# Inverse DFT over W of a two-layer convolution block: even frequencies by the parity of k2 over a quarter of the row, sums on GpSimd

## Chip, cores and metric

The kernel runs on one core of one Trainium2 chip. The metric is the device time of one execution in microseconds (us). All arithmetic is in float32. TensorE is called PE in the profile (its weight loads are listed apart as PEld), VectorE is DVE, ScalarE is ACT, GpSimd is POOL, SyncE is SP.

## The reference

The input `x` is a batch of 4 images of 512 x 512 pixels with 16 channels. Two layers are applied, each to a group-normalised copy of its input and with a residual sum.

```python
# layer 0
X = rfft2(gn(x), s=(1024, 1024));  Y = einsum('...hwi,ijhw->...hwj', X, H_full)
x = x + irfft2(Y, s=(1024, 1024))[..., :512, :512, :]
# layer 1
x = x + conv3x3_cosine_arccos(gn(x))      # 3x3, 16 to 16 channels, divided by norms
```

`H_full` is a filter made from two small polynomials. Only the last transform of layer 0 matters here: the inverse DFT over W. It turns 512 complex frequencies per image row (of a transform of length 1024) into 512 real pixels.

## The kernel before

The work goes through five phases in order of time: the filter (`filter_phase`, with the statistics of the first normalisation beside it), the forward transform over W, the mixing of channels per frequency (`conv_phase`, by far the longest), and then `last_phase`. This starts with the stage that the change touches, the inverse DFT over W, and goes on with layer 1.

**The stage.** It is the `with ExitStack() as inner` block of `last_phase`, and it makes 256 tiles of 128 rows by 512 pixels. The outer loop over `n` (16 steps) loads eight inputs `yt0` to `yt7` of 1 MB each through SP's DMA queue, from two buffers per input (`i_y`, `bufs=2`), so the loads for step n+2 wait until PE has done with step n. The inner loop over `m` (16 steps) makes one tile. The frequencies lie in eight chunks of 128, which are cosine chunks kc = 0 to 3 and sine chunks kc = 4 to 7; in each four the first two are even frequencies `2*k2` (with k2 sorted into even and odd ones) and the last two are odd frequencies.

The tile is made from the symmetry about the middle of the row. Eight matmuls (L1141) of 128 x 128 weights, which are the data, by 128 x 256 moving columns, which are the constant `inv`, put the sum over cosines in `po[:, 0]` and the sum over sines in `po[:, 1]`, each for the left half of the row. ACT copies the sine half to SBUF (L1146, `od`). DVE adds the two plus a bias for the left half (L1148), and subtracts them for the right half, written backwards (L1149). ACT's queue then issues the store of the tile to the DRAM array `yw_d` (L1153). `po` has four PSUM buffers, `od` and `yo` four SBUF buffers.

**The work beside it.** The generator `prepare` reads the result back for the second normalisation. One place of it is a 128 x 128-pixel patch: it loads the patch of the original image (`p_x`, 1 MB) and of `yw_d` (`p_y`, two halves of 0.5 MB), adds them on POOL (L1071, two additions per place), takes statistics on DVE (L1067, 16 instructions per place), and stores the sum to `t_d` (1 MB). There are 64 places, 16 per image. A place of image 0 needs rows that steps n = 0 to 7 of the stage write. In the program's text, `next(beside)` is called from step n = 9 on, and later once per unit of layer 1; a scheduler then lays all instructions out in one fixed order per engine, and moves places forward where it believes an engine to be free. An engine executes its own queue strictly in that order.

**Layer 1.** It has 256 units of 128 rows x 32 columns. Each uses PE (L1183, L1209, L1279, L1287), ACT (L1191 to L1315), DVE (L1297, L1331 to L1334) and POOL (L1320, L1325, L1339) in turn; the remaining places of `prepare` run in between. L1339 runs once per unit and so counts the units in the trace.

Of the kernel before, what the change touches and what calls it, by code (L numbers as in the profile page):

```python
# [40 lines left out]
F32 = mybir.dt.float32  # L41
AF = mybir.ActivationFunctionType
ALU = mybir.AluOpType
AX = mybir.AxisListType
PSUM = bass.MemoryType.PSUM

P = 128
N = 512
# [22 lines left out]
def constants():  # L71

    c = {}
# [21 lines left out]
    for cc in range(2):  # L95
        taps = (back * (1, 1j)[cc]).reshape(N, S, 8)
        for plane in range(2):
            v = np.einsum("kse,sr->kre", (taps.real, taps.imag)[plane], over_s)
# [8 lines left out]
    for r in range(33):  # L107
# [5 lines left out]
        for part in range(2):  # L113
# [6 lines left out]
            else:  # L120
                v = -(sig.real @ np.sin(f_all))
# [16 lines left out]
    a = fwd.reshape(2, 4, P, 2, P).transpose(4, 3, 1, 0, 2).copy()  # L138
# [5 lines left out]
    own = np.pad(own, ((0, 0), (0, 9 * 64 - own.shape[1]))).reshape(2, 9, 64)  # L144
    c["own"] = np.tile(own.transpose(1, 0, 2).reshape(-1), (P, 1))
    inv = fwd * np.where(f > 0, 2.0, 1.0)[:, None] / (2 * N)
    c["inv"] = inv.reshape(8, P, 256).transpose(1, 0, 2).reshape(P, -1)
    c["ident"] = np.eye(P)

    def turn(n, of):  # L150
# [15 lines left out]
    for s0 in range(4):  # L166
        for cx in range(2):
            for c2 in range(2):
                n = gg[:, None] * s0 + 4 * gg[:, None] * s1[None, :] + 32 * (cx + c2)
# [20 lines left out]
def load_const(nc, pool, cst, name, shape=None):  # L190
    src = cst[name]
    t = pool.tile(list(src.shape), F32, name=f"c_{name}")
    nc.sync.dma_start(out=t, in_=src)
    return t


def dram(t, row, offset, *dims):

    pitch = t.shape[1]
    lead = [[pitch, t.shape[0]]] if row is None else []  # L200
    return bass.AP(tensor=t.tensor, offset=t.offset + (row or 0) * pitch + offset,
                   ap=lead + [list(d) for d in dims])
# [759 lines left out]
def last_phase(tc, cst, x, y_d, yw_d, t_d, kern, bias, radius, out):  # L962
    nc = tc.nc
    with ExitStack() as ctx:
# [22 lines left out]
        bias_y = cp.tile([P, 1], F32, name="l_bias_y")  # L987
# [132 lines left out]
        with ExitStack() as inner:  # L1120
            ip = inner.enter_context(tc.tile_pool(name="i_const", bufs=1))
            yp = inner.enter_context(tc.tile_pool(name="i_y", bufs=2))
            op = inner.enter_context(tc.tile_pool(name="i_o", bufs=4))
            ps = inner.enter_context(tc.tile_pool(name="i_ps", bufs=4, space=PSUM))
            inv = load_const(nc, ip, cst, "inv").rearrange("p (k n) -> p k n", k=8)
            for n in range(16):
                b2, half, s8 = n // 8, n // 4 % 2, n % 4
                yt = []
                for kc in range(8):
                    t = yp.tile([P, 4, 2, 2, P], F32, name=f"yt{kc}")  # L1130
                    at = (64 * half + 32 * (kc // 4) + 16 * b2 + 4 * s8) * 4 * P
                    nc.sync.dma_start(
                        out=t.rearrange("p a o h x -> p (a o h x)"),
                        in_=dram(y_d[kc % 4], None, at, [1, 16 * P]),
                    )
                    yt.append(t)
                for m in range(16):
                    s1, odd, bh = 4 * s8 + m // 4, m // 2 % 2, m % 2
                    po = ps.tile([P, 2, 256], F32, name="po")
                    for kc in range(8):  # L1140
                        nc.tensor.matmul(  # L1141
                            po[:, kc // 4], yt[kc][:, m // 4, odd, bh, :], inv[:, kc, :],
                            start=(kc % 4 == 0), stop=(kc % 4 == 3),
                        )
                    od = op.tile([P, 256], F32, name="od")
                    nc.scalar.copy(od, po[:, 1])  # L1146
                    o = op.tile([P, N], F32, name="yo")
                    nc.vector.scalar_tensor_tensor(o[:, :256], po[:, 0], bias_y, od, ALU.add, ALU.add)  # L1148
                    nc.vector.scalar_tensor_tensor(o[:, 256:][:, ::-1], po[:, 0], bias_y, od,  # L1149
                                                   ALU.add, ALU.subtract)  # L1150

                    h0 = 8 * (4 * s1 + 2 * half + odd)
                    nc.scalar.dma_start(out=yw_d[2 * bh + b2][:, h0 : h0 + 8, :], in_=o)  # L1153
                    if n >= 9 and m % 2 == 1:
                        next(beside, None)
# [232 lines left out]
def body(tc, ins, cst, out):  # L1388
    g_d = [tc.dram_tile([P, G_ROW + PITCH], F32, name=f"g_d{r}") for r in range(4)]
    x_d = [tc.dram_tile([P, X_ROW + PITCH], F32, name=f"x_d{r}") for r in range(4)]  # L1390
    y_d = [tc.dram_tile([P, Y_ROW + PITCH], F32, name=f"y_d{r}") for r in range(4)]
    yw_d = [tc.dram_tile([C, N, N], F32, name=f"yw_d{b}") for b in range(B)]
    t_d = [[tc.dram_tile([N, P, C], F32, name=f"t_d{b}_{w}") for w in range(4)] for b in range(B)]
    with tc.tile_pool(name="s_mv", bufs=2 * B) as mp:
        mvs = []
        with tc.tile_pool(name="s_in", bufs=1) as xp:
            beside = image_stats(tc, xp, mp, ins["x"], mvs)
            filter_phase(tc, cst, ins["L0_conv_h0"], ins["L0_conv_numerators"][0],
                         ins["L0_conv_denumerator"], g_d, beside)
            for _ in beside:  # L1400
                pass
        forward_phase(tc, cst, ins["x"], mvs, x_d)
    conv_phase(tc, cst, g_d, x_d, y_d)
    last_phase(tc, cst, ins["x"], y_d, yw_d, t_d, ins["L1_conv_kernel"], ins["L1_conv_bias"],
               ins["L1_conv_radius"], out)
# [6 lines left out]
def build(inputs, body=body):  # L1412
    import concourse.bacc as bacc

    nc = bacc.Bacc("TRN2", target_bir_lowering=False, num_devices=1)
    arrays, ins, cst = {}, {}, {}
    for name in _INS:
        a = np.ascontiguousarray(inputs[name])
        arrays[f"in_{name}"] = a
        ins[name] = nc.dram_tensor(f"in_{name}", a.shape, F32, kind="ExternalInput").ap()  # L1420
    for name, a in constants().items():
        arrays[f"k_{name}"] = a
        cst[name] = nc.dram_tensor(f"k_{name}", a.shape, F32, kind="ExternalInput").ap()
    out = nc.dram_tensor("out", (B, N, N, C), F32, kind="ExternalOutput").ap()
    with tile.TileContext(nc) as tc:  # L1425
        body(tc, ins, cst, out)
    return nc, arrays
# [8 lines left out]
```

## Times and profile before

| what | value |
|---|---|
| median of 3 runs | 16473.95 us (16464.4 to 16498.5) |
| profiled execution, its own time | 16489.29 us |
| span of the profiled execution | 16487.4 us, granted PE clock 0.972 |
| PE busy in the span | 15039.9 us (91%) |
| first and last L1141 matmul | 13694.0 us and 14696.4 us |
| L1141 | 4096 instructions (two per float32 matmul), 923.0 us busy |
| L1148 and L1149 on DVE | 256 each, 480 and 475 ns |
| L1146 on ACT | 256, 372 ns |
| L1071 on POOL, 128 x 1024 | 128, 2848 ns |
| L1067 on DVE, 128 x 128 | 1024, 366 ns |
| first and last L1339 | 14780.8 us and 16481.6 us |

The page gives busy times over the whole span, where the stage is only 6% of it. The stage is therefore read from answers of the trace for stretches of time: busy time of each engine in each stretch, the granted PE clock, the busy share of the DMA engines, the waits by what ended them, and the timelines of single engines. A busy time of a matmul includes the tail of the pipeline, so the pace of a run of matmuls is read from the starts of neighbouring groups and not from the mean duration of one.

### The profile page before, as it was taken

Reading aid. Unit: us, or ns where it says so; the run is one execution under the profiler, and the core shown is the slowest. Engines: PE = TensorE matmul, PEld = TensorE weight load, DVE = VectorE, ACT = ScalarE, POOL = GpSimd, SP = SyncE. Lnnn points to the kernel's source line nnn. Section 1 sums busy time; section 2 is a strip of 40 time slices with the busy share of each in tenths; the row PEclk is TensorE's granted clock in tenths of the full one; section 3 lists DMA queues with packets and bytes.
Section 4 is the critical chain, followed back from the end, with each engine's and each line's share of the span. In section 5 each row is a group of like instructions: output and inputs, shape, how many; then the busy total and the mean of one; then the engine's idle time right before and its main releaser. Section 6 shows DMA issues by size and latency. Waiting matters only on the chain. (4 is left out here: it accounts for less than half of the span.)

```text
span 16487.4 us, 538106 instructions
## 1 busy us (share of the span) xinstructions
PE 15039.9 (91%) x232588; PEld 11221.5 (68%) x232588; DVE 10549.6 (64%) x20763; ACT 8870.6 (54%) x17007; POOL 10203.4 (62%) x9645
## 2 busy tenths in 40 slices
PE   7999999999988889898988899888889998988898
PEld 5555555554567777677777777777777777777787
DVE  8999999974545555555555555555555552447877
ACT  4666666653345555555555555555555551027888
POOL 7777777763356666666666666666666660237766
PEclk8999999999999999999999999999999999989999
DMA  4888888888888888888888888888888886885531
GB/s 139 241 244 247 240 243 248 240 244 250 251 282 328 324 326 330 317 327 329 328 329 317 326 328 327 317 318 324 324 326 329 326 321 232 313 279 167 167 110 67
DMA packets 2914640, 4542.92 MB, mean 276 GB/s; under 512 B 126114, under 2 KB 2094460, under 8 KB 2801422
## 3 DMA queue, kind: packets, MB, share of 16 engines
q1 hardware_dynamic: 2703070, 3836.37, 67.9%
q0 software_dynamic: 172336, 605.00, 9.5%
q10 hardware_dynamic: 36864, 67.13, 1.2%
q8 instruction: 1833, 30.03, 0.7%
q14 instruction: 537, 4.40, 0.1%
HBM read 3030.71 MB, written 1477.31 MB: 273 GB/s over the span
## 5 line engine op out<-in xcount | busy, mean ns | idle before, releaser
L828 PE MATMUL pg<-c_dg,g 64*128 64x128 f32 x32832 | 2838.7, 290 | 344.4 <-ACT gh L728 192.2
L844 PE MATMUL pm<-xe,gh 128*32 128x64 f32 x131328 | 2380.2, 222 | 520.0 <-issue 299.3
L844 PEld LDWEIGHTS pm<-xe,gh 128*32 128x32 f32 x131328 | 2001.1, 110 | 1113.6 <-issue 891.7
L828 PEld LDWEIGHTS pg<-c_dg,g 64*128 64x128 f32 x32832 | 2277.5, 189 | 690.3 <-issue 248.1
L873 DVE TENSOR_TENSOR z<-zq,pz 128x256 f32<-128x256 f32 x2052 | 859.5, 419 | 2634.6 <-ACT zq L872 2567.4
L726 DVE COPY gh<-pg 128x512 f32<-128x512 f32 x2046 | 1408.2, 688 | 1208.9 <-PE pg L828 1205.8
L458 PE MATMUL pt<-ev_in,c_todd 128*128 128x512 f32 x4096 | 1927.5, 609 | 16.2 <-DMA ev_in<-g_d 16.2
L797 POOL TENSOR_TENSOR xu<-xe,c_late 128x256 f32<-128x256 f32 x2052 | 1391.7, 702 | 808.5 <-ACT xe L728 791.2
L388 DVE RECIPROCAL dn<-dn 128x256 f32<-128x256 f32 x1024 | 1722.8, 1724 | 17.6
L728 ACT COPY yf<-pm 128x512 f32<-128x512 f32 x2046 | 1211.4, 592 | 886.9 <-PE pm L844 873.2
L389 POOL TENSOR_TENSOR sp<-m,dn 128x512 f32<-128x512 f32 x1024 | 1300.9, 1271 | 592.4 <-DVE dn L388 552.0
L808 ACT COPY xe<-xl 64x1024 f32<-64x1024 f32 x513 | 538.7, 1050 | 1877.9 <-POOL xl L799 1877.8
L728 ACT COPY gh<-pg 128x512 f32<-128x512 f32 x2058 | 1200.2, 583 | 368.8 <-PE pg L828 365.7
L865 PE MATMUL pz<-c_ident,yf 128*128 128x128 f32 x8208 | 1371.7, 290 | 24.2 <-issue 10.8
L458 PEld LDWEIGHTS pt<-ev_in,c_todd 128*128 128x128 f32 x4096 | 728.2, 190 | 920.6 <-issue 792.3
L417 ACT COPY st<-pg 128x256 f32<-128x256 f32 x2048 | 616.8, 391 | 1301.5 <-PE pg L406 1301.3
L406 PEld LDWEIGHTS pg<-c_dinv,sp 64*128 64x128 f32 x16384 | 1005.5, 196 | 442.2 <-ACT sp L394 232.6
L799 POOL TENSOR_TENSOR xl<-xl,xu 128x1024 f32<-128x1024 f32 x513 | 1209.5, 2358 | 40.2
L406 PE MATMUL pg<-c_dinv,sp 64*128 64x128 f32 x16384 | 1108.2, 287 | 60.2 <-ACT sp L394 44.6
L881 POOL TENSOR_TENSOR zd<-z 128x512 f32<-128x512 f32 x513 | 653.7, 1274 | 765.4 <-DVE z L873 765.3
L1279 PE MATMUL pc<-l_band,xn 128*128 128x160 f32 (+2 forms) x6144 | 1076.2, 333 | 51.7 <-DVE e_o L1334 51.7
L913 POOL DMA_DIRECT2D y_d<-yo x511 | 296.5, 580 | 1325.0 <-ACT yo L728 1299.8
(211 smaller groups left out, 30193.2 us busy)
## 6 DMA issues: line engine op xcount, KB each, us to landing
xe<-xf_d SPq DMA_DIRECT2D x1026, 1536.0 KB
g<-g_d SPq DMA_DIRECT2D x511, 1024.0 KB
g_d<-st SPq DMA_DIRECT2D x256, 1024.0 KB
ev_in<-g_d SPq DMA_DIRECT2D x1024, 256.0 KB
g_d<-ot SPq DMA_DIRECT2D x1024, 256.0 KB
xf_d<-xe POOLq DMA_DIRECT2D x513, 448.0 KB, 8.2
xf_d<-xl POOLq DMA_DIRECT2D x513, 448.0 KB, 5.4
x_d<-xo SPq DMA_DIRECT2D x128, 1024.0 KB
```

Source lines behind the costliest of these rows:

```text
L388: nc.vector.reciprocal(dn, dn)
L389: nc.gpsimd.tensor_mul(w["sp"][:, v], w["m"][:, v], bc(dn, 2, [P, 2, 2, P]))
L406: nc.tensor.matmul(pg[u][:, n, k].rearrange("p a x -> p (a x)"), w["sp"][q, n, k, c, :], dinv[q, 2 * kp + k, c, :], start=(c == 0), stop=( ...
L458: nc.tensor.matmul(pt, todd[:, c, kc, hh * P : hh * P + P], ev[:, kc, c], start=(kc == 0), stop=(kc == 1),)
L726: nc.vector.tensor_copy(dst, src)
L728: nc.scalar.copy(dst, src)
L797: nc.gpsimd.tensor_mul(u[:, :, h, c], xe[:, :, h, 1 - c], bc(late[:, 1 + c], 2, [P, F, 2]))
L799: nc.gpsimd.tensor_add(xl.rearrange("p f h c k -> p (f h c k)"), xl.rearrange("p f h c k -> p (f h c k)"), u.rearrange("p f h c k -> p (f ...
L828: nc.tensor.matmul(pg[c][:, j % 4], g[half, j], dg[half], start=True, stop=True)
L844: nc.tensor.matmul(pm[32 * q : 32 * q + 32, g % 8], gh[:, f].rearrange("p c j -> p (c j)"), xe[:, :, f].rearrange("p t h c k -> p t (h c k ...
L865: nc.tensor.transpose(pz[:, t % 4].rearrange("p v q x -> p (v q x)"), y[:, at].rearrange("p g x -> p (g x)"), ident)
L1279: nc.tensor.matmul(pc[:, lo:hi, :].rearrange("p w j -> p (w j)"), xns[q][:, h * P + dh : h * P + dh + P], bands[dh][:, o : o + hi - lo, :] ...
```

## The change

The constant `inv` is split into an odd part, for both halves of the 256 columns, and an even part, for the first 128 columns only. The left half of the row is cut once more about its own middle: of the even frequencies, those with even k2 repeat mirrored and those with odd k2 repeat mirrored with the opposite sign (for cosines, and the other way round for sines). So 128 columns are computed for each parity.

Per tile there are now four matmuls of 128 columns, each by itself (`pe`, four results of 128 columns: parity by cosine or sine), and four of 256 columns for the odd frequencies (`po`, two results accumulated over two chunks). ACT copies all of `pe` to SBUF (`ye`, 512 columns). POOL adds and subtracts the two parities (`yq`, two instructions of 256 columns). DVE adds the odd sums in `po` to `yq` in place (512 columns), and then makes the tile with two instructions of 256 columns as before, which read `yq` from SBUF. The odd part of the constant and the second quarter of the even results are stored mirrored, so the output pattern has two stretches of 128 columns per instruction. `pe` and `po` have three PSUM buffers each, `ye` and `yq` three SBUF buffers each, `yo` keeps four.

```diff
     inv = fwd * np.where(f > 0, 2.0, 1.0)[:, None] / (2 * N)
-    c["inv"] = inv.reshape(8, P, 256).transpose(1, 0, 2).reshape(P, -1)
+    inv = inv.reshape(2, 4, P, 2, P).transpose(2, 0, 1, 3, 4).copy()
+    inv[:, :, 2:, 1] = inv[:, :, 2:, 1, ::-1]
+    inv[:, 1, 2:, 1] *= -1
+    c["inv"] = np.concatenate([inv[:, :, 2:].reshape(P, -1), inv[:, :, :2, 0].reshape(P, -1)], 1)
...
-            op = inner.enter_context(tc.tile_pool(name="i_o", bufs=4))
-            ps = inner.enter_context(tc.tile_pool(name="i_ps", bufs=4, space=PSUM))
-            inv = load_const(nc, ip, cst, "inv").rearrange("p (k n) -> p k n", k=8)
+            op = inner.enter_context(tc.tile_pool(name="i_o", bufs=3))
+            ps = inner.enter_context(tc.tile_pool(name="i_ps", bufs=3, space=PSUM))
+            inv = load_const(nc, ip, cst, "inv")
+            odd_m = inv[:, : 4 * 256].rearrange("p (v k n) -> p v k n", v=2, k=2)
+            even_m = inv[:, 4 * 256 :].rearrange("p (v k n) -> p v k n", v=2, k=2)
...
+                    pe = ps.tile([P, 2, 2, P], F32, name="pe")
                     po = ps.tile([P, 2, 256], F32, name="po")
-                    for kc in range(8):
-                        nc.tensor.matmul(
-                            po[:, kc // 4], yt[kc][:, m // 4, odd, bh, :], inv[:, kc, :],
-                            start=(kc % 4 == 0), stop=(kc % 4 == 3),
-                        )
-                    od = op.tile([P, 256], F32, name="od")
-                    nc.scalar.copy(od, po[:, 1])
-                    o = op.tile([P, N], F32, name="yo")
-                    nc.vector.scalar_tensor_tensor(o[:, :256], po[:, 0], bias_y, od, ALU.add, ALU.add)
-                    nc.vector.scalar_tensor_tensor(o[:, 256:][:, ::-1], po[:, 0], bias_y, od,
+
+                    def row_of(kc):
+                        return yt[kc][:, m // 4, odd, bh, :]
+
+                    for k in range(2):
+                        for v in range(2):
+                            nc.tensor.matmul(pe[:, k, v], row_of(4 * v + k), even_m[:, v, k], start=True, stop=True)
+                    for v in range(2):
+                        for k in range(2):
+                            nc.tensor.matmul(po[:, v], row_of(4 * v + 2 + k), odd_m[:, v, k],
+                                             start=(k == 0), stop=(k == 1))
+                    e = op.tile([P, 2, 2, P], F32, name="ye")
+                    nc.scalar.copy(e, pe)
+                    q = op.tile([P, 2, 2, P], F32, name="yq")
+                    nc.gpsimd.tensor_add(q[:, :, 0], e[:, 0], e[:, 1])
+                    nc.gpsimd.tensor_sub(q[:, :, 1], e[:, 0], e[:, 1])
+                    nc.vector.tensor_add(q.rearrange("p v h x -> p v (h x)"), po, q.rearrange("p v h x -> p v (h x)"))
+                    o = op.tile([P, N], F32, name="yo", bufs=4)
+                    o4 = o.rearrange("p (a b x) -> p a b x", a=2, b=2)
+                    nc.vector.scalar_tensor_tensor(o4[:, :, 0], q[:, 0], bias_y, q[:, 1], ALU.add, ALU.add)
+                    nc.vector.scalar_tensor_tensor(o4[:, ::-1, 1, ::-1], q[:, 0], bias_y, q[:, 1],
                                                    ALU.add, ALU.subtract)
```

In the changed kernel these lines are L1152 (matmuls of 128 columns), L1155 (256 columns), L1158 (copy on ACT), L1160 and L1161 (POOL), L1162, L1165 and L1166 (DVE), L1170 (store) and L1074 (the additions of `prepare`).

## The prediction

> **What bounds the kernel now.** The page comes first: PE is busy for 91% of the span, but the change touches one stage of about 1000 us (first to last L1141 matmul, 13694 to 14697). So I read stretches of time there: busy time of PE, PEld, DVE, ACT and POOL with instruction counts, then PE clock, DMA busy share and GB/s.
>
> ```profile
> span 16487.4 us, 538106 instructions
> ...
> 13760.00:13820.00 60.00, 60.00 (x280) 52.82 (x279) 15.76 (x36) 6.37 (x18) 0.00 (x0) 1.00 0.66 245
> ...
> 13694.00:14005.00 311.00, 308.36 (x1410) 268.95 (x1411) 75.88 (x174) 32.50 (x88) 0.00 (x0) 0.99 0.69 259
> 14005.00:14180.00 175.00, 175.00 (x812) 154.06 (x812) 61.10 (x164) 18.47 (x50) 26.16 (x10) 1.00 0.80 286
> 14180.00:14697.00 517.00, 439.92 (x1881) 373.77 (x1879) 232.64 (x695) 44.71 (x118) 149.96 (x54) 0.93 0.92 323
> ```
>
> Up to 14180 PE has no gap: 812 instructions in 175 us are 216 ns each, and the timelines of ACT and DVE repeat every 3.455 us, which is 16 x 216 ns: a tile. PE bounds this part. From 14180 on PE has 1881 instructions in 517 us, 4.40 us per tile, at a DMA share of 0.92. The waits of 14040 to 14720 say why (who waited for what: us, times, longest):
>
> ```profile
> ACT od L1146 <- DVE yo L1149: 307.3, 83, 13.0
> POOL p_x L1071 <- DMA p_x<-in_x: 268.1, 23, 34.0
> DVE l_stats L1067 <- POOL p_x L1071: 196.1, 47, 11.9
> POOL p_x L1071 <- DMA p_y<-yw_d: 178.1, 8, 50.3
> ...
> PE po L1141 <- DVE yo L1149: 66.8, 22, 6.2
> ```
>
> Read from the bottom: PE waits for DVE to free `po`, DVE waits in its queue for POOL's addition, POOL for loads. So the second part is bound by transfers, through an in-order chain. Between tile 90 (14005, first addition) and the end the trace has 66 additions, 33 places:
>
> ```profile
> 14005.30 5.65 POOL L1071 TENSOR_TENSOR p_x<-p_x,p_y 128x1024 f32<-128x1024 f32 x2 [357.12 <-DMA p_y<-yw_d]
> 14059.70 2.83 POOL L1071 TENSOR_TENSOR p_x<-p_x,p_y 128x1024 f32<-128x1024 f32 x1 [48.75 <-DMA p_y<-yw_d]
> ```
>
> Layer 1 receives what leaves the stage. L1339 runs once per unit; L1071 is the work beside it:
>
> ```profile
> L1339 POOL TENSOR_TENSOR e_o<-e_o,xt x114: 1255/1273/1303, 15010.4 to 15794.4; 128x512 f32<-128x512 f32 x114
> ...
> L1071 POOL TENSOR_TENSOR p_x<-p_x,p_y x46: 2818/2873/2917, 15006.4 to 15758.6; 128x1024 f32<-128x1024 f32 x46
> ...
> L1339 POOL TENSOR_TENSOR e_o<-e_o,xt x92: 1261/1272/1289, 15810.3 to 16394.2; 128x512 f32<-128x512 f32 x92
> ```
>
> With places beside it a unit takes 784.0/113 = 6.94 us, without 583.9/91 = 6.42. So 113 x 0.52 = 59 us for 23 places: 2.6 us per place.
>
> **What the Trainium skill says.** "TensorE: Matmul & The Clock Gate", section "Back-to-back issue gap": the spacing of load and matmul pairs "is set by *both* ops, pipelined". The trace agrees: each weight load is listed with 190 ns, yet this run of 128-column instructions starts at 15513.27 and the next at 15514.14, 0.87/8 = 109 ns apart:
>
> ```profile
> 15513.27 1.04 PE L1183 MATMUL pt<-c_ident,xt 128*128 128x128 f32 x8
> 15514.14 0.59 PE L1279 MATMUL pc<-l_band,xn 128*128 128x512 f32 x1
> ```
>
> "GPSIMD Engine Reference", section "1. Specifications": its SBUF interfaces are shared with VectorE, with contention from DVE instructions that have two SBUF inputs. The new L1165 and L1166 are such; no row of before shows the contention in this stage, where L1148 has one PSUM input. "DMA: Bandwidth & Descriptors", section "Issuing engines are not separate DMA queues": SP's loads and ACT's stores share the same DMA engines. The share of 0.92 with both running fits.
>
> **The change part by part, per tile.**
>
> *PE.* Removed: 16 instructions x 216 = 3.455 us. Added: 8 of 256 columns x 216 = 1.73 and 8 of 128 columns x 109 = 0.87, together 2.60; I take 2.62. The L1183 pace is of transposes; bounds for a matmul are 108 ns (half of 216) and 190 ns (the whole load exposed): 2.59 to 3.25 per tile.
>
> *ACT.* The copy grows from 372 ns to the 592 of L728 (512 columns from PSUM). Its queue also holds the store, 525 ns. Sum 1.1 us, under 2.62. The copies stand two tiles ahead of the stores in ACT's queue in the built program, so a store waiting for DVE doesn't stop the next copy.
>
> *POOL.* New: two instructions of 256 columns, 702 ns each (L797), 1.40 us; without contention 0.65 (half of L881's 1274), with it perhaps double, 2.8, which would be just over PE's pace. I take 1.40, hidden under PE.
>
> *DVE.* One addition of 512 columns from PSUM, 682 ns (L1297), and two of 256, 475 each as now, since only the input moves to SBUF (bounds 400, the pace in the timeline, and 950): 1.63 us instead of 0.96. Hidden as well.
>
> *Buffers.* From the last `pe` matmul to a free `po`: copy 0.6, POOL 1.4, addition 0.7, some 3 us with the waits, of which 1.73 lie under the `po` matmuls. Three buffers are 7.9 us, so nothing stops PE while nobody upstream waits.
>
> *Order.* The changed POOL queue has 43 additions, 21.5 places, up to the last tile instead of 66, because POOL has work now. 11.5 places go to layer 1, with their loads, stores and 16 DVE instructions each. And the tile's sums now stand behind L1071 in POOL's queue: when that waits for a load, the sums, DVE, `po` and PE wait after some 5 us of cover (two tiles). DVE's queue had this wait already, through L1067. Constants 256 KB smaller: nothing. SP's loads of `yt` stand in the same queue as before, with fewer places in between.
>
> **The sum.** First part, tiles 0 to 89: 90 x (3.455 - 2.62) = 75 us gained. DMA allows it: the share of 0.66 at 3.455 us is 2.28 us of DMA work per tile, 0.87 at the new pace, under 0.92.
>
> Second part, 166 tiles, 692 us now. DMA work there is 0.80 x 175 + 0.92 x 517 = 616 us. By bytes a tile's 2.28 are 1.52 for loads (8.4 MB per 16 tiles) and 0.76 for its store (0.26 MB). Two steps are loaded ahead, so eight steps remain: 128 x 1.52 + 166 x 0.76 = 321. The rest, 295, is 8.9 us per place. With 21.5 places: 321 + 191 = 512 us of DMA work; at the mean share of this part now, 616/692 = 0.89, that is 575 us. PE needs 166 x 2.62 = 435, so transfers stay the bound. Gain 692 - 575 = 117.
>
> Given back: 11.5 places x 2.6 = 29 us in layer 1; bounds 0 (all under other work) and 65 (5.65 us of POOL each, if POOL's time lies on the path). Last, the first four places: in the changed queue their additions stand behind the sums of tiles 90, 106, 122 and 138, where the data come now (14005 is tile 90, ten tiles or 34 us after step 4 was written). At 2.62 us 34 us are 13 tiles, so POOL waits three tiles, 8 us, less 5 of cover: 4 x 3, I take 8 in all.
>
> Sum: -75 - 117 + 29 + 8 = -155 us. The profiled execution took 16489.3 (its span and 2 us around it), so 16334; it stands 15 us over the median of 16474, to which I apply the same: 16319.
>
> **The rivals.**
> - *The chain eats the second part.* POOL's waits keep the 692 us as they are, and only the first part gains: -75 + 29 + 8 = -38, 16436. For it: two engines now stand in line for each load. Against it: the DMA share is 0.92, so work taken away shortens it.
> - *Fewer transfers count for more.* Share 0.95 in the second part: 512/0.95 = 539, and nothing given back: -75 - 153 = -228, 16246. For it: layer 1 has a DMA share of 0.5. Against it: DVE is over 80% busy there.
> - *128-column matmuls pay the whole load.* 3.25 us per tile: the first part gains 18, the second 117 still (540 of PE is under 575): -18 - 117 + 37 = -98, 16376. Against it: the 109 ns.
> - *Slower: serial waits.* Between 14040 and 14720 POOL waited 268 + 178 + 63 (for `yw_d`) = 509 us for 32 places, 15.9 us per place. If the tile loop stands still for each such wait and makes its tiles only between, the stage takes 236 + 435 + 21.5 x 15.9 = 1013 instead of 1003; with 65 given back, +75: 16549. It decides from 14 us of standstill per place. Against it: waits overlap with tiles as long as buffers last, and the long ones are mostly times in which POOL is early.
>
> **How the numbers follow.** The forecast has 0.54 (on its own 16275 to 16375), the first rival 0.16, the second 0.14, the third 0.08, the slower one 0.08. Half of the second rival lies under 16250; over 16435 lie the slower one and a third of the first: 0.2 outside 16250 to 16435. A measurement of this kernel tells about 0.2%, 33 us, from no change. Faster: 0.54 + 0.14 + 0.08 + 0.11 = 0.87; within: 0.05 of the first and 0.02 of the slower rival, 0.07; slower 0.06.
>
> **What would show it.** In the profile after: tiles before the first L1074 at 2.6 us (ACT copies 2.6 apart; 3.2 for the third rival); then about 3.5 us per tile at a DMA share near 0.9 (if 4.2 with POOL's waits at the head: first rival; if the share falls under 0.8 with PE waiting for DVE: the slower one); some 800 us from first to last matmul; units of layer 1 at 6.9 us in their first 140. The forecast is wrong if POOL's L1160 takes over 1.2 us, or if the places given back lengthen layer 1 by more than 65 us.

## The result and the profile after

The changed kernel took 16375.0 us, median of 4 runs (16333.8 to 16398.1), against 16483.3 us for the kernel before on the same chip (4 runs, 16464.4 to 16498.5): ratio 0.9936, 95% interval 0.9923 to 0.9949. That is 108 us less, where 155 was forecast. The profiled execution is the longest of the four, 16398.1 us with a span of 16396.3; against the span before it is 91 us shorter. In pieces, read from the first and last instruction of the lines named (before, after):

| piece | before | after | difference | forecast |
|---|---|---|---|---|
| start to first matmul of the stage | 13694.0 | 13699.5 | +5.5 | 0 |
| stage, first to last matmul | 1002.4 | 840.4 | -162.0 | -184 |
| last matmul to first L1339 (L1356 after) | 84.4 | 67.0 | -17.4 | 0 |
| layer 1, first to last L1339 (L1356) | 1700.8 | 1783.7 | +82.9 | +29 |

With -0.1 in the tail they sum to -91.1. The stage came out near the forecast; layer 1 gave back nearly three times what was counted. First the stage, in stretches (engines, PE clock, DMA share, GB/s as before):

```profile
13760.00:13820.00 60.00, 58.62 (x352) 53.14 (x351) 39.01 (x67) 12.88 (x22) 32.12 (x45) 1.00 0.84 311
13699.50:13955.00 255.50, 248.43 (x1484) 226.38 (x1485) 165.28 (x268) 53.09 (x91) 132.91 (x181) 0.98 0.86 318
13955.00:14540.00 585.00, 472.50 (x2617) 423.91 (x2616) 441.04 (x844) 97.44 (x166) 359.54 (x369) 0.91 0.89 310
```

At 13955 the first addition of the read-back starts, behind POOL's sums of tile 89, the ninetieth; PE is then 1484/16, nearly 93 tiles, on. The first part has the pace forecast, as PE's timeline shows from the starts of neighbouring groups: 0.89 us for eight instructions of 128 columns, 1.73 for eight of 256.

```profile
13803.82 1.05 PE L1152 MATMUL pe<-c_inv,yt 128*128 128x128 f32 x8
13804.71 1.89 PE L1155 MATMUL po<-c_inv,yt 128*128 128x256 f32 x8
13806.44 1.05 PE L1152 MATMUL pe<-c_inv,yt 128*128 128x128 f32 x8
```

The second part takes 585 us at a DMA share of 0.89. PE has 2617 instructions there, 164 tiles, which would take 429 us at 2.62 us each; it is busy for 472.5 us, at a granted clock of 0.91 (429/0.91 = 471), and idle for the other 112. The waits from 13955 to 14540 (who waited for what: us, times, longest) look different from those of before: what PE and ACT wait for most is DVE and POOL, and POOL hardly waits for loads.

```profile
ACT ye L1158 <- POOL yq L1161: 123.3, 20, 12.5
PEld po L1155 <- DVE yq L1162: 112.0, 32, 9.5
PE po L1155 <- DVE yq L1162: 106.0, 31, 9.3
ACT ye L1158 <- DVE yo L1166: 96.6, 40, 12.2
...
POOL p_x L1074 <- DMA p_x<-in_x: 33.9, 10, 7.2
```

Layer 1, with units counted by L1356 and the additions beside them:

```profile
L1356 POOL TENSOR_TENSOR e_o<-e_o,xt x144: 1257/1276/1328, 14606.9 to 15690.2; 128x512 f32<-128x512 f32 x144
...
L1074 POOL TENSOR_TENSOR p_x<-p_x,p_y x84: 2751/2878/2919, 14612.8 to 15670.3; 128x1024 f32<-128x1024 f32 x84
L1074 POOLq EVENT_SEMAPHORE  x47: 17/43/11605, 14612.2 to 15664.6; - x47
its engine sat idle before it (us, times) until:
  DMA p_x<-in_x: 64.9, 19
  issue: 34.9, 9
```

143 intervals in 1083.3 us are 7.58 us per unit, where 6.9 was forecast. POOL stood idle 65 + 35 = 100 us in front of additions (the "issue" part is idle time that the profile puts down to nothing). The same query of before, over its layer 1:

```profile
L1071 POOL TENSOR_TENSOR p_x<-p_x,p_y x61: 2818/2872/2931, 14784.3 to 15758.6; 128x1024 f32<-128x1024 f32 x61
L1071 POOLq EVENT_SEMAPHORE  x15: 17/43/2377, 14789.0 to 15751.1; - x15
its engine sat idle before it (us, times) until:
  DMA p_x<-in_x: 22.9, 10
  issue: 2.3, 2
```

25 us there. The theory after this profile: most of the extra length of layer 1 comes not from the number of places, but from additions that stand at the head of POOL's in-order queue before their loads have landed. The rival is the forecast's own reading, a price per place, only higher (some 7 us each). For the stage the theory of the prediction was that transfers bound the second part; the rival is the chain of POOL and DVE.

### The profile page after: what moved, and what is told of

Read it like the earlier page. It is cut to its first block, busy times and chain, and to the rows that moved or that the text cites. A ratio compares the mean times of both kernels' runs of the same rounds, so it can differ in the third digit from the quotient of the medians.

```text
span 16396.3 us, 539024 instructions
## 1 busy us (share of the span) xinstructions
PE 14868.9 (91%) x232588; PEld 11093.9 (68%) x232588; DVE 10839.5 (66%) x21019; ACT 8930.2 (54%) x17007; POOL 10584.5 (65%) x10157
```

## The experiments

All times are set against the kernel before, run on the same chip beside each of them (medians 16461 to 16481). A stage is given from its first to its last matmul, layer 1 from its first to its last L1339 or its counterpart, both from the profile.

**Places held in order, without and with the change.** A chain of order-only dependencies runs over the POOL instructions of `next(beside)` and one instruction of each unit of layer 1, so the scheduler can't move an addition ahead of the unit where the program's text has it. Against the tiles of the stage, which are not in the chain, additions can still move. In the orders of both built programs 36 additions, 18 places, then stand ahead of layer 1, and 46 places in it.

```diff
+        chained = InOrder(tc, nc.gpsimd)
...
-                        next(beside, None)
+                        with chained:
+                            next(beside, None)
...
-                gate(u + 1)
+                with chained:
+                    gate(u + 1)
...
-                next(beside, None)
+                with chained:
+                    next(beside, None)
```

> The kernel before, with POOL's additions of the read-back held in the program's own order against layer 1, so that 18 places stand in the stage instead of 33 and the other 15 run beside layer 1. If a place costs layer 1 the 2.6 us of the prediction, the stage falls from 1003 to PE's 256 x 3.455 = 885 us and layer 1 gains 39: some 80 us faster than before. If late places cost layer 1 about 7 us each, as the profile after suggests (83 us longer for some 12 places), layer 1 grows by 105 and the whole is within 20 us of before.

> The changed kernel with the same hold, so the same 18 places in the stage as in the held kernel before it. Its stage against that one is the change alone, without moved places. Transfers as the only bound of the second part: stage about 790 us (840 less 3.5 places of 8.9 us, less the waits), layer 1 9 us longer. If late places cost 7 us: 25 us longer in layer 1. In the whole within 30 us of the changed kernel, and 80 to 100 us faster than the held kernel before.

Measured: the held kernel before 16364.7 us (ratio 0.9930, 0.9913 to 0.9947), stage 945.0, layer 1 1679.8. The held changed kernel 16241.7 (ratio 0.9859, 0.9844 to 0.9873), stage 830.2, layer 1 1680.6. The price per place falls in both forms: layer 1 is shorter than in either unheld kernel although it has more places beside it. So the rival, some 7 us for each late place, is out: it asked for 105 us more in the held kernel before, and layer 1 came out 21 us shorter. In both held kernels the additions in layer 1 have no idle time of POOL in front of them at all; the changed one:

```profile
L1074 POOL TENSOR_TENSOR p_x<-p_x,p_y x92: 2809/2876/2926, 14573.8 to 15549.1; 128x1024 f32<-128x1024 f32 x92
L1074 POOLq EVENT_SEMAPHORE  x43: 17/43/43, 14613.8 to 15537.5; - x43
its engine sat idle before it (us, times) until:
who waited for it (us, times):
  DVE l_stats L1070: 7.6, 3
```

1680 us plus the wait gives 1705 for before (1701 measured) and 1780 after (1784 measured). The sum leaves out the number of places, which is 31, 42 and 46 in the kernels before, after and held; what the places' own work costs is measured below. With the same 18 places ahead of layer 1, the change alone is worth 16364.7 - 16241.7 = 123 us, of which the stage has 115. The stage of the held kernel before missed its expectation of 885 by 60: PE is idle for 36 us there before matmuls that wait for DVE to free `po`, so 18 places cost the stage before the change something too. The held changed kernel missed as well: its stage is 830 and not 790, and it is 133 us faster than the changed kernel, where at most 30 were expected.

**Sums on DVE, without the hold.** Is it POOL's new work that spoils layer 1?

```diff
-                    nc.gpsimd.tensor_add(q[:, :, 0], e[:, 0], e[:, 1])
-                    nc.gpsimd.tensor_sub(q[:, :, 1], e[:, 0], e[:, 1])
+                    nc.vector.tensor_add(q[:, :, 0], e[:, 0], e[:, 1])
+                    nc.vector.tensor_sub(q[:, :, 1], e[:, 0], e[:, 1])
```

> The changed kernel without the hold, sums on DVE. In its order 44 additions stand before layer 1, as many as with the sums on POOL. If layer 1 grew because additions stand in POOL's queue before their loads have landed, the waits of L1074 in layer 1 (100 us in the changed kernel) and its length (1784) come back here, 60 us or more over the held kernels' 1680, whatever engine makes the sums. If POOL's extra work of the stage was the reason, layer 1 is near 1700.

Measured: 16359.9 us (ratio 0.9932, 0.9918 to 0.9947), stage 810.4, layer 1 1784.7, with POOL idle for 101 us in front of additions there.

```profile
L1074 POOL TENSOR_TENSOR p_x<-p_x,p_y x85: 2800/2877/2934, 14558.2 to 15626.6; 128x1024 f32<-128x1024 f32 x85
L1074 POOLq EVENT_SEMAPHORE  x52: 17/43/6706, 14588.0 to 15620.9; - x52
its engine sat idle before it (us, times) until:
  DMA p_x<-in_x: 68.1, 21
  issue: 33.0, 10
```

A third point near the same line: 1680 + 101 = 1781. The engine of the sums doesn't matter for it. And since 44 additions stand ahead of layer 1 here, the prediction's reason for the move from 66 to 43 ("because POOL has work now") was wrong.

**Transfers taken away.** In the held changed kernel the stage's inputs are loaded for two steps only and reused, so the other tiles are made from the wrong rows.

```diff
-                yt = []
-                for kc in range(8):
+                if n > 1:
+                    yt = yts[n % 2]
+                else:
+                    yt = []
+                    yts.append(yt)
+                for kc in range(8) if n < 2 else ():
```

> The held changed kernel, in which the inputs of the stage are loaded for the first two steps only and reused by the other fourteen (their tiles are then made from the wrong rows): 117 MB less to load. If transfers bound the second part, the stage falls to PE's pace, 256 x 2.62 = 671 plus some 20 us. If the chain of POOL, DVE and PE bounds it, places still cost: 730 us or more from first to last matmul.

Measured: 16229.5 us (ratio 0.9849, 0.9834 to 0.9863), stage 793.9. 117 MB less shorten the stage by 36 us only, so transfers are not its only bound. The trace shows one thing that stops it. POOL's and DVE's timelines, around two additions of the read-back:

```profile
14084.08 0.73 POOL L1167 TENSOR_TENSOR yq<-ye 128x256 f32<-128x256 f32 x1
14087.08 5.74 POOL L1074 TENSOR_TENSOR p_x<-p_x,p_y 128x1024 f32<-128x1024 f32 x2 [2.28 <-DMA p_x<-in_x]
14092.78 0.91 POOL L1166 TENSOR_TENSOR yq<-ye 128x256 f32<-128x256 f32 x1
```

```profile
14085.01 0.47 DVE L1172 SCALAR_TENSOR_TENSOR yo<-yq,l_bias_y 128x256 f32<-128x256 f32 x1
...
14087.50 2.70 DVE L1171 SCALAR_TENSOR_TENSOR yo<-yq,l_bias_y 128x256 f32<-128x256 f32 x1
14090.13 2.98 DVE L1172 SCALAR_TENSOR_TENSOR yo<-yq,l_bias_y 128x256 f32<-128x256 f32 x1
14093.03 1.74 DVE L1070 BATCH_NORM_STATS2 l_stats<-p_x 128x6 f32<-128x128 f32 x6
```

DVE's output instruction, 0.47 us by itself, takes 2.70 and 2.98 us, each as long as one of POOL's two additions beside it. PE's gap there ends with DVE's next addition:

```profile
14095.42 3.46 PE L1161 MATMUL po<-c_inv,yt 128*128 128x256 f32 x8 [5.01 <-DVE yq L1168]
```

The gap costs more than its 5.01 us: the eight instructions after it take 3.46 us, where eight such took 1.89 in the part without gaps, and the granted PE clock of that stretch (third figure from the end) is 0.55:

```profile
14095.40:14099.00 3.60, 3.58 (x10) 2.91 (x11) 3.60 (x11) 0.59 (x1) 1.58 (x3) 0.55 0.99 389
```

**One SBUF input per output instruction.** Half of the sum goes back into PSUM; the second output instruction is changed like the first.

```diff
-                    nc.vector.tensor_add(q.rearrange("p v h x -> p v (h x)"), po, q.rearrange("p v h x -> p v (h x)"))
+                    s = po.rearrange("p v (h x) -> p v h x", h=2)
+                    nc.vector.tensor_add(s[:, 0], s[:, 0], q[:, 0])
+                    nc.vector.tensor_add(q[:, 1], s[:, 1], q[:, 1])
...
-                    nc.vector.scalar_tensor_tensor(o4[:, :, 0], q[:, 0], bias_y, q[:, 1], ALU.add, ALU.add)
+                    nc.vector.scalar_tensor_tensor(o4[:, :, 0], s[:, 0], bias_y, q[:, 1], ALU.add, ALU.add)
```

> The held changed kernel, with DVE's addition split: one half of the sum goes back into PSUM, so that each of the two output instructions has one SBUF input, as before the change, at the price of a second addition (475 ns each instead of one of 682, 0.27 us more of DVE per tile). If DVE's instructions with two SBUF inputs stand still while POOL works, the output instructions return from 841 and 641 ns to about 480, and the stage shortens by 30 us or more. If transfers bound the stage, its length stays within 10 us.

Measured: the output instructions return to 480 and 476 ns, from 802 and 624 in the held changed kernel (the last figure before the second bar is the mean of one; first the held changed kernel, then this one):

```profile
L1166 DVE SCALAR_TENSOR_TENSOR yo<-yq,l_bias_y 128x256 f32<-128x256 f32 x256 | 205.4, 802 | 48.8 <-DMA yw_d<-yo 43.1
L1167 DVE SCALAR_TENSOR_TENSOR yo<-yq,l_bias_y 128x256 f32<-128x256 f32 x256 | 159.7, 624 | 0.0
...
L1168 DVE SCALAR_TENSOR_TENSOR yo<-po,l_bias_y,yq 128x256 f32<-128x256 f32 x256 | 123.0, 480 | 68.3 <-DMA yw_d<-yo 63.5
L1169 DVE SCALAR_TENSOR_TENSOR yo<-po,l_bias_y,yq 128x256 f32<-128x256 f32 x256 | 122.0, 476 | 0.0
```

The longest of these 512 takes 494 ns, although 39 of them run beside one of POOL's long additions. The stage is 810.3, 20 us shorter, less than the 30 expected; the whole, 16249.2 (ratio 0.9862, 0.9847 to 0.9877), can't be told from the held changed kernel. So the mechanism is there; its price in the stage is about 20 us, net of the second addition (429 and 421 ns for the two, instead of 681 for the one).

**POOL's additions cut** to 4 of 128 columns (the rest of each patch stays the original image, in result and statistics).

```diff
-                    part = t[:, :, 8 * jh : 8 * jh + 8]
-                    nc.gpsimd.tensor_add(part, part, ys[jh].rearrange("p j w -> p w j"))
+                    part = t[:, :4, 8 * jh : 8 * jh + 8]
+                    nc.gpsimd.tensor_add(part, part, ys[jh].rearrange("p j w -> p w j")[:, :4])
```

> The held changed kernel, in which each addition of the read-back covers 4 of 128 columns only (the rest of the patch stays the original image, in the result and in its statistics); loads, statistics and stores stay. POOL gets back nearly 5.7 us per place, and DVE's output instructions have little left to wait for. If POOL's additions stop the tiles in the second part, the stage falls from 830 to 740 us or less. If the transfers bound it, it stays over 800.

Measured in one run: 16147.3 us, stage 782.6, layer 1 1616.1. Both expectations missed: 47 us less in the stage, but far from PE's pace. From 14100 to 14400 the DMA share is 0.93 to 0.95, so here transfers can be what bounds; the next run takes both away. Layer 1 is 64.5 us shorter than in the held changed kernel, as the first and last L1358 show, here and then there:

```profile
L1358 POOL TENSOR_TENSOR e_o<-e_o,xt x256: 1259/1276/1312, 14523.8 to 16139.9; 128x512 f32<-128x512 f32 x128
...
L1358 POOL TENSOR_TENSOR e_o<-e_o,xt x256: 1258/1276/1327, 14570.4 to 16251.0; 128x512 f32<-128x512 f32 x128
```

Neither kernel has a wait in front of an addition there, so 64.5/46 = 1.4 us is what the work of POOL's additions costs layer 1 per place. It is a price per place, only a smaller one than the forecast's 2.6.

**Both cuts, then the statistics too.** The held changed kernel with loads for two steps and short additions; and the same with 2 of 16 statistics per place, the others set to a constant (so the second normalisation differs).

> The held changed kernel with both cuts: inputs loaded for two steps only, and additions of the read-back over 4 of 128 columns (results are then not the reference's). Each cut alone gave 794 and 783 us for the stage. If transfers and POOL's additions are the two limits of the second part, neither is left, and the stage is at PE's pace, 671 us and at most 30 more. If something else stops the tiles (DVE's statistics, stores), it stays over 740.

```diff
-                    for j in range(8 * jh, 8 * jh + 8):
+                    if h == 0 and w == 0:
+                        nc.vector.memset(stats, 1.0)
+                    for j in range(8 * jh, 8 * jh + 1):
```

> The held changed kernel with both cuts, and in addition only 2 of the 16 statistics per place (the others are set to a constant, so the normalisation is not the reference's). 18 places x 14 x 0.29 us, 73 us of DVE time less in the stage. If DVE's statistics between the tiles' instructions are what keeps the kernel with both cuts 86 us above PE's pace, the stage falls from 757 to 700 us or less. If it stays over 735, the chain of copy, sums and outputs itself cannot follow PE.

Measured in one run each: 16125.6 us and stage 756.8 with both cuts, 16115.6 and stage 758.6 with the statistics cut too. Neither comes near PE's pace. DVE's statistics are not the cost. What is left is in one stretch; PE's instructions (first bracket) and the DMA share (last but one) of the last kernel:

```profile
13700.00:13900.00 200.00, 200.00 (x1225) 184.29 (x1223) 143.25 (x231) 44.56 (x76) 111.84 (x151) 1.00 0.45 127
13900.00:14000.00 100.00, 91.19 (x537) 82.61 (x536) 68.10 (x122) 19.35 (x33) 49.96 (x73) 0.98 0.56 164
14000.00:14100.00 100.00, 85.32 (x482) 77.14 (x481) 58.11 (x100) 18.18 (x31) 45.98 (x70) 0.93 0.76 231
14100.00:14200.00 100.00, 77.15 (x411) 68.56 (x409) 50.54 (x90) 14.66 (x25) 40.47 (x66) 0.90 0.91 302
14200.00:14300.00 100.00, 92.58 (x542) 83.83 (x543) 76.34 (x137) 20.52 (x35) 52.71 (x76) 0.98 0.68 210
14300.00:14400.00 100.00, 100.00 (x615) 92.17 (x614) 73.91 (x118) 22.28 (x38) 58.18 (x78) 1.00 0.39 102
```

Before and after the places PE runs at 613 instructions per 100 us, 2.61 us per tile: copy, sums and outputs do follow PE, against the expectation's last clause. Between, while the places' own loads and stores come together, it falls to 411. The 1972 instructions from 13900 to 14300 would take 322 us at that pace; PE is idle for 54 us and busy for 346, so 24 us more go to its lower clock (0.90 to 0.98). The waits there (DVE's statistics for POOL's addition 73 us, POOL's additions for loads, stores and unnamed causes 89, PE for DVE 48) point to loads that are late at the head of the two queues; since no kernel left the places' loads out, this stays argued.

**Places spread out.** Patches taken row by row, called from step 5 on, with and without the split addition.

```diff
-            places = [(b, w, h) for b in order for w in range(4) for h in range(4)]
+            places = [(b, w, h) for b in order for h in range(4) for w in range(4)]
...
-                    if n >= 9 and m % 2 == 1:
+                    if n >= 5 and m % 4 == 3 or n >= 12 and m % 4 == 1:
```

> The held changed kernel with the places of an image taken row by row of patches, and so spread from step 5 on, about one per 12 tiles, instead of four per step late. If places cost because several come close together and outrun two tiles of cover, the stage shortens by 20 us or more. If each costs by itself, it stays at 830.

> The spread kernel with the split addition (one SBUF input per output instruction). Against the spread kernel: 20 us less in the stage, as the split gave before (830 to 810), if the time that DVE's two-input instructions lose to POOL's long additions adds up with the rest.

Measured: 16272.0 us (ratio 0.9881, 0.9865 to 0.9898) and stage 828.4; with the split addition 16263.1 (0.9873, 0.9858 to 0.9888) and stage 810.2. The whole is no faster than the held changed kernel, and layer 1 is a little longer (1693 and 1685). The trace shows that the edit did not do what it was meant to: the first addition starts 234 us after the first matmul, instead of 255 in the held changed kernel, and from there to the end of the stage 19 places stand as unevenly as the 18 before (8 follow the last within 20 us, in both). So whether places cost singly or because they come close together stays open. The split is worth 18 us again.

**Sums on DVE, held.** The same edit as above, on the held changed kernel.

> The held changed kernel with the two sums of the parities on DVE instead of POOL. DVE then has about 2.5 us per tile beside PE's 2.62, and no tile waits in POOL's queue. If the wait behind additions in POOL's queue is the cost of the second part, the stage shortens in spite of DVE's load (under 815 us); if the time that DVE and POOL take from each other is the cost, it gets longer (850 us or more), since DVE has four more instructions with SBUF inputs only to lose, and its statistics come on top.

> The held kernel with the sums on DVE again, now timed: 16235, some 5 to 15 us less than the held kernel with the sums on POOL (16242), if the single look holds.

Measured: 16234.4 in a single run; then 16237.8 from four (ratio 0.9857, 0.9840 to 0.9873), stage 805.5 and 808.4 (the two profiles of one kernel differ by 3 us). The tiles no longer queue behind POOL's additions, and the stage is 22 to 25 us shorter although DVE has two instructions more per tile. In the whole it equals the held changed kernel. Both beat the kernel before and the changed one.

## Why the prediction was right or wrong

*Direction and size.* Faster was right; of 155 us, 108 came by the medians and 91 in the profiled execution.

*PE per tile.* Right: 2.62 us forecast, 2.62 in the timeline. The pace of transposes (109 ns) held for matmuls of 128 columns (0.89/8 = 111 ns), though each weight load is listed with over 190. The third rival is out.

*First part.* Nearly right. In its 255 us PE ran 1484 instructions, nearly 93 tiles, which take 243 at the pace forecast. Of the 12 us more, 9 lie in the first 60 us, with 312 PE instructions instead of some 367 and a granted clock of 0.92. The prediction put the boundary at tile 90; in the kernel before PE had run 1410 instructions by 14005, 88 tiles, which changes this term by under 2 us.

*Second part.* The term (575 us and 8 for early additions) met the 585 measured, but its reason, "transfers stay the bound", does not stand alone. Without 117 MB of transfers the stage shortens by 36 us, not to PE's pace. POOL's additions alone are worth 47, both together 73, and 86 more above PE's 671 come with the places in some other way, in part as PE's lower clock. That the formula fitted is in part luck: the DMA share of 0.89, which it took over from before, already held such waiting. The prediction also gave PE 2.62 us per tile throughout. At the clock granted there (0.91) PE's 164 tiles kept it busy for 472.5 us and not for 429, so a gap of PE can cost twice, as idle time and as slower matmuls after it.

*"Given back: 11.5 places x 2.6 = 29 us in layer 1".* This step failed: +83. The number of places was right (61 additions in layer 1 before, 84 after). The price was not: the prediction divided a difference in pace by a number of places, and put longer waits at nothing. The held kernels have 46 places in layer 1 and need 1680 us, 21 less than before with 31. What lengthens it most is idle time of POOL in front of additions: 25 us before, 100 after, 0 held, 101 with the sums on DVE, and layer 1 took 1701, 1784, 1680 and 1785. Of the 83 us, 75 are more of this wait; 11.5 places at the 1.4 us that POOL's work costs (shortened additions) would be 16. The two make 91, so neither term is exact; nor is 1680 plus the wait, which counts no places. How many places the scheduler moves was read from the order; where in layer 1 it puts them was not looked at, nor whether their loads could have landed. The upper bound of 65 for this term assumed work and not waiting, and was passed: by the sign that the prediction itself named, its account of layer 1 was wrong, although the total came near.

*"Because POOL has work now".* Wrong, as the order with the sums on DVE shows. What makes the scheduler move fewer places was not settled.

*Contention of DVE and POOL.* The prediction cited the Trainium skill, "GPSIMD Engine Reference", section "1. Specifications", and bounded DVE's outputs at 950 ns. The mean of L1165 was 841 ns, inside; but single ones take 2.7 us and more, as long as POOL's instruction. The trace agrees with the page that two SBUF inputs are what matters: with one input moved to PSUM the mean is 480. The prediction took 475; the difference cost about 20 us of stage, as the split addition shows.

*POOL's sums.* 0.70 us forecast each, 0.76 and 0.77 measured: right.

*The slower rival* came true in kind, since tiles did queue behind additions in POOL's queue (123 us of ACT's waits), but not in size.

*Not foreseen.* The gap between stage and layer 1 is 17 us shorter; in the held kernel before it is 32 shorter without the change, so the order of the read-back alone can shorten it. In the held kernels with the change it lies between 52 and 66 us; why is open.

## What to carry to other kernels

When a change shortens a stage in which a scheduler hides later work, read the new order at the place where that work lands, and ask of each instruction on an in-order queue whether its load can have arrived: idle time at the head of a queue, more than the amount of work, set the price here. Fixing the order of such filler work was worth as much (116 us by the medians beside it) as the cut in matmuls (108 us by itself), and both together gave 239. Before sums are moved to GpSimd, look for long GpSimd instructions in the same stretch: in this kernel they delayed the sums queued behind them, and they held up VectorE instructions with two SBUF inputs.

## What the runs showed of the hardware

A VectorE `scalar_tensor_tensor` of 128 x 256 float32 with two SBUF inputs takes 0.47 us by itself, up to 1.05 us beside GpSimd sums of 256 columns, and 2.70 or 2.98 us beside a GpSimd addition of 2.8 us. With one PSUM and one SBUF input it stays at 0.48 beside the same additions. GpSimd loses less: its sums go from 0.72 to about 0.91 us. In the changed kernel, beside sums of POOL and then without:

```profile
13808.86 1.05 DVE L1165 SCALAR_TENSOR_TENSOR yo<-yq,l_bias_y 128x256 f32<-128x256 f32 x1
13809.83 0.47 DVE L1166 SCALAR_TENSOR_TENSOR yo<-yq,l_bias_y 128x256 f32<-128x256 f32 x1
```

Matmuls that follow a gap of PE can run at a lower granted clock: after 5.01 us of idle time eight instructions of 256 columns took 3.46 us at a clock of 0.55, where eight without a gap took 1.89. In the second part of the stage PE was busy for 472.5 us with work of 429 us, at a mean clock of 0.91.
